# Cross-attention on one Trainium2 core: where the transposition of the probabilities, the third remainder and the key and value loads stand in each slot's order

## Chip, core and metric

The kernel runs on one core of one Trainium2 chip. The metric is the device time of one execution in microseconds (us). TensorE is called PE below (its weight loads PEld), VectorE is DVE, ScalarE is ACT, GpSimd is POOL, and SyncE, which here only issues DMAs, is SP.

## The reference

Only one layer of what the reference sets up is live: cross-attention of `x` (32 batches of 512 rows of 640 channels) with the 77 context rows of each batch, 20 heads of 32 channels, a softmax over the 77 keys, an output projection, a bias and a residual. The three other key sets have no rows here (the context ends at row 77), so they add nothing.

```python
ehs_txt = encoder_hidden_states[:, :77]
q = _heads(hidden_states @ to_q_w)
h_txt = _sdpa(q, _heads(ehs_txt @ to_k_w), _heads(ehs_txt @ to_v_w))
out = _merge(h_txt) @ to_out_w + to_out_b
out = out + hidden_states
```

All of it is float32. The kernel splits each operand into a high part (rounded to the type that PE takes) and a low part (the remainder), and adds up high x high, high x low and low x high.

## The kernel before

A first stage (about the first 300 us) makes keys and values of all batches and puts them into DRAM (`k_dram`, `v_dram`). The main stage is 160 slots, five for each of the 32 batches. Slot `n = 5 b + j` treats chunk `j` of batch `b`: 128 channels, which are four heads. Below, "slot 0" to "slot 4" are the five values of `j`. The order of the instructions is written out by hand: each engine runs its own in the order of the program, and so does SP with the DMAs.

What one slot does:

- **Scores.** Four times (`t` = 0 to 3, 128 query rows each) PE makes scores for four heads (L367: one matmul with the high queries and two with arranged copies, `qt` slots 1 and 2, of low and high halves), and DVE takes the negated row maximum (L375, `nm`). Score banks are three deep. `exps` (L385) has ACT make sixteen exponentials in four groups of four, with row sums.
- **Queries of the next slot.** PE makes them in two parts (L332; 6 and 9 matmuls) into the single bank `pq`. `split_q` has ACT copy the high part (L343) and then two half copies of it from SBUF (L347); DVE subtracts to get the low part (L349, two instructions), which waits for L343 alone. The next slot's second and third score matmuls need L349; the bank `pq` is free only after it.
- **Probabilities of the slot before.** DVE makes reciprocals of the sums (L395), POOL multiplies (`normalize`, L400), DVE transposes in blocks of 32 into `z` (`transpose_p`, L407; one buffer), and SP writes `z` to DRAM with four DMAs (L414, `pd<-z`). One slot later `load_p` reads it back with two DMAs (L423, L424, `raw<-pd`), which completes the transposition. So L407 of a slot waits until the four `pd<-z` of the slot before have landed, and `load_p` waits for the same.
- **Values, three slots behind** (`taken`). ACT casts the loaded probabilities to the high part (`cast_p`, L431) and a third tile of 64 rows (`rest_p`, L437); DVE subtracts for the low part (L438), POOL for the third tile (`last_p`, L445). PE then makes eight matmuls (`values`, L459): the first needs L431, the second L438, the last two L437 and L445. `split_a` splits the result on ACT and DVE (L104, L105).
- **Output projection of an earlier batch**: twice twelve matmuls (`piece`, L489). `finish` has DVE add a closed half to the residual (L517), and SP write a row block out (L521) when both halves are closed. Residuals are loaded by L478, the bias is added by POOL (L482).
- **Loads.** `refill` loads keys in slots 0 and 2 (L309 and L312, eight DMAs) and values in slots 1 and 3 (L319, seven DMAs), half of them at the slot's start and half after `load_p`. In slot 4 `load_x` loads the `x` of the batch after next (L267, four DMAs). `x` is transposed on DVE (L272) and split on ACT and POOL (L279, L280) in slots 2 and 3.

Where the change touches it, the order before is, engine by engine:

- SP: first half of the refill; `load_p`; second half; `out` of the first `finish`; `load_x` (slot 4); residual; four `pd<-z`; `out` of the second `finish`.
- POOL: `normalize`; `last_p`; bias; splits of `x`.
- DVE: maximum 0; L438; L395; maximum 1; L517; maximum 2; **L407; L349 twice**; maximum 3; L517; L105.
- ACT: L431; L437; exponentials 0; exponentials 1; L343; L347 twice; exponentials 2; splits of `x`; L104; exponentials 3.

The program gives its DMAs eight completion semaphores in turn. An issue on SP waits until the transfer that was issued eight places before it has landed, whatever that one was.

Of the kernel before, what the change touches and what calls it, by code (L numbers as in the profile page):

```python
# [35 lines left out]
SEGMENTS = []  # L36
# [14 lines left out]
def kernel(  # L51
# [251 lines left out]
    def load_keys(b, g, heads=range(HPC)):  # L303
        j0, nj = GROUPS[g]
        kb, kc = kbs[g]
        src = k_dram[:, j0 : j0 + nj, :, b * NKEY : (b + 1) * NKEY].bitcast(F32)
        for i in heads:
            r, half = slice(i * HD, (i + 1) * HD), i % 2 * NKEY
            nc.sync.dma_start(  # L309
                kb[r, :, i * NKEY : (i + 1) * NKEY].bitcast(F32), src[r, :, i // 2, :]  # L310
            )
            nc.sync.dma_start(kc[r, :, :, half : half + NKEY].bitcast(F32), src[r])  # L312

    def load_values(b, g, segments=SEGMENTS):
        j0, nj = GROUPS[g]
        v = v_dram.rearrange("n (j i) d a -> n j i (d a)", i=HPC)
        for t, r0, i, k0, kn in segments:
            k0 += b * NKEY
            nc.sync.dma_start(  # L319
                vbs[g][r0 : r0 + kn, :, t, i * HD : (i + 1) * HD, :]  # L320
                .rearrange("p j d a -> p j (d a)")
                .bitcast(F32),
                v[k0 : k0 + kn, j0 : j0 + nj, i, :].bitcast(F32),
            )
# [28 lines left out]
    def scores(n, t):  # L353
        b, j = divmod(n, NC_)
        g = GROUP_OF[j]
        qt, (kb, kc) = qts[n % 2], kbs[g]
        jg = j - GROUPS[g][0]
        sc = ps.tile([P, S], F32, tag="sc", name="sc", bufs=3)
        half = KCOLS // 2
        for m, (cols, keys_) in enumerate(  # L360
            (
                (slice(0, KCOLS), kb[:, jg]),
                (slice(0, half), kc[:, jg, 0]),
                (slice(half, KCOLS), kc[:, jg, 1]),
            )
        ):
            nc.tensor.matmul(  # L367
                sc[:, cols],
                qt[:, m, t * P : (t + 1) * P],
                keys_,  # L370
                start=(m == 0),
                stop=(m == 2),
            )
        nm = main.tile([P, HPC], F32, tag="nm", name="nm", bufs=3)
        nc.vector.tensor_reduce(  # L375
            nm, sc[:, :KCOLS].rearrange("p (h k) -> p h k", k=NKEY), AX.X, ALU.max, negate=True
        )
        return sc, nm

    def exps(n, t, sc, nm):  # L380
        if t == 0:
            sms[n] = main.tile([P, NQ * HPC], F32, tag="sm", name="sm", bufs=2)
        for i in range(HPC):
            at = t * HPC + i
            nc.scalar.activation(  # L385
                pnb[n % 2][:, at, :NKEY],
                sc[:, i * NKEY : (i + 1) * NKEY],
                AF.Exp,
                bias=nm[:, i : i + 1],
                accum_out=sms[n][:, at : at + 1],  # L390
            )

    def sums(n):
        rs = main.tile([P, NQ * HPC], F32, tag="rs", name="rs", bufs=2)
        nc.vector.reciprocal(rs, sms.pop(n))  # L395
        return rs

    def normalize(n, rs):
        pf = pnb[n % 2][:, :, :NKEY]
        nc.gpsimd.tensor_tensor(  # L400
            pf, pf, rs.unsqueeze(2).to_broadcast([P, NQ * HPC, NKEY]), ALU.mult
        )

    def transpose_p(n):

        pn = pnb[n % 2]
        nc.vector.transpose(  # L407
            z.rearrange("p b t j -> p t b j"),
            pn.rearrange("p (t h) k -> p t (h k)", t=NQ).rearrange("p t (b i) -> p t b i", i=Q),
        )  # L410
        pd = dram.tile([NBLK * Q, S], F32, tag="pd", name="pd", bufs=6)
        rows = pd.rearrange("(b i) q -> i b q", i=Q)
        for a in range(4):
            nc.sync.dma_start(  # L414
                rows[:, :, a * P : (a + 1) * P],
                z[a * Q : (a + 1) * Q].rearrange("p b t j -> p b (t j)"),
            )
        pds[n] = pd
# [8 lines left out]
    def cast_p(n):  # L427

        raw = raws[n]
        pp = late[0].tile([P, 5, S], FPR, tag="pp", name="pp", bufs=1)  # L430
        nc.scalar.copy(pp[:, 0:2, :], raw[:, 0:2, :])  # L431
        pps[n] = pp

    def rest_p(n):

        raw, pp = raws[n], pps[n]
        nc.scalar.copy(pp[:64, 4, :], raw[:64, 2, :])  # L437
        nc.vector.tensor_tensor(  # L438
            pp[:, 2:4, :], raw[:, 0:2, :], pp[:, 0:2, :].bitcast(F32), ALU.subtract
        )  # L440

    def last_p(n):

        raw, pp = raws.pop(n), pps[n]
        nc.gpsimd.tensor_tensor(  # L445
            pp[64:, 4, :], raw[:64, 2, :], pp[:64, 4, :].bitcast(F32), ALU.subtract
        )
# [27 lines left out]
    def load_residual(b, t, xr=None):  # L475
        if xr is None:
            xr = late[0].tile([P, C], F32, tag="xr", name="xr", bufs=3)
        nc.sync.dma_start(xr, x[b, t * P : (t + 1) * P, :])  # L478
        xrs[b, t] = xr
# [31 lines left out]
    def finish():  # L511

        while closed:
            b, t, h = closed.pop(0)
            xr = xrs[b, t]
            cols = slice(h * HALF, (h + 1) * HALF)
            nc.vector.tensor_tensor(  # L517
                xr[:, cols], pos.pop((b, t, h))[:, :HALF], xr[:, cols], ALU.add
            )
            if h == 1:  # L520
                nc.sync.dma_start(out[b, t * P : (t + 1) * P, :], xr)  # L521
# [18 lines left out]
        values(m)  # L540
        split_a(m)

    def refill(b, j, part):

        heads = range(2 * part, 2 * part + 2)
        segments = SEGMENTS[4 * part : 4 * part + 4]
        if j == 0:
            load_keys(b, 1, heads)
        elif j == 1:
            load_values(b, 0, segments)  # L550
        elif j == 2 and b + 1 < B:
            load_keys(b + 1, 0, heads)
        elif j == 3:
            load_values(b, 1, segments)

    def slot(n, beside=None):
        b, j = divmod(n, NC_)
        ahead, more = n + 1 < N, b + 1 < B
        back, first = PIECES[j]
        bo_, has_out = b - back, b >= back  # L560
        xsplits = SPLIT_X.get(j, ((), ())) if more else ((), ())
        turns = TRANSPOSE_X.get(j, ((), (), ())) if more else ((), (), ())
        taken, second = takes.get(n), seconds.get(n)

        refill(b, j, 0)
        if taken is not None:
            cast_p(taken)
        s = scores(n, 0)
        if taken is not None:
            rest_p(taken)  # L570
        if n:
            normalize(n - 1, sums(n - 1))
        if taken is not None:
            last_p(taken)
        exps(n, 0, *s)
        if ahead:
            queries(n + 1, 0, 2)
        s = scores(n, 1)
        if n - LAG + 1 in pds and n > LATE:
            load_p(n - LAG + 1)  # L580
        refill(b, j, 1)
        finish()
        if j == 4 and b + 2 < B:
            load_x(b + 2)
        if j in RESIDUAL and b >= RESIDUAL[j][0]:
            load_residual(b - RESIDUAL[j][0], RESIDUAL[j][1])
        if j in BIAS and b >= BIAS[j][0]:
            add_bias(b - BIAS[j][0], BIAS[j][1])
        exps(n, 1, *s)
        for i in turns[0]:  # L590
            transpose_x(b + 1, i)
        if ahead:
            queries(n + 1, 2, NC_)
        s = scores(n, 2)
        if n:
            transpose_p(n - 1)
        if ahead:
            split_q(n + 1)
        exps(n, 2, *s)
        for c in xsplits[0]:  # L600
            split_x(b + 1, c)
        if has_out:
            piece(bo_, first)
        if taken is not None:
            values(taken)
        if beside:
            beside()
        s = scores(n, 3)
        finish()
        for i in turns[1]:  # L610
            transpose_x(b + 1, i)
        if taken is not None:
            split_a(taken)
        for c in xsplits[1]:
            split_x(b + 1, c)
        exps(n, 3, *s)
        if has_out:
            piece(bo_, first + 1)
        for i in turns[2]:
            transpose_x(b + 1, i)  # L620
        if second is not None:
            cast_p(second)
            rest_p(second)
            last_p(second)
            take(second)
            if second + 2 in pds and second + 2 not in takes.values():
                load_p(second + 2)
# [141 lines left out]
```

## Time and profile before

| | us |
|---|---|
| three runs | 2018.67, 2020.97, 2023.04 |
| median | 2020.97 |
| the profiled execution, its own time | 2018.67 |
| its span, first to last instruction | 2016.9 |

The granted clock of TensorE was 0.989 over the span. The page of the profile gives these busy shares:

| engine | busy us | share of the span | instructions |
|---|---|---|---|
| PE | 1963.4 | 97% | 11012 |
| PEld | 1763.5 | 87% | 11012 |
| ACT | 1588.0 | 79% | 6377 |
| DVE | 1354.7 | 67% | 2159 |
| POOL | 981.9 | 49% | 617 |

The DMA queue of SP moved 421.10 MB, its packets took 82.4% of sixteen engines' span. Durations used below are mean times of one instruction or, where stated, start times in a stretch of the timeline; all times are from the start of the span.

| line, engine | what | count | mean ns |
|---|---|---|---|
| L407 DVE | `z<-pn` | 160 | 1511 |
| L349 DVE | `qt<-pq,qt` | 320 | 670 |
| L375 DVE | `nm<-sc` | 640 | 460 |
| L438 DVE | `pp<-raw,pp` | 160 | 1226 |
| L400 POOL | `pn<-pn,rs` | 160 | 2278 |
| L445 POOL | `pp<-raw,pp` | 160 | 1309 |
| L431 ACT | `pp<-raw` | 160 | 1063 |
| L347 ACT | `qt<-qt` | 320 | 619 |

### The profile page before, as it was taken

What the parts mean: (1) busy time and instruction counts of PE and PEld (TensorE: products, weight loads), DVE (VectorE), ACT (ScalarE), POOL (GpSimd) and SP (SyncE); (2) the same over time, 40 slices, a digit from 0 to 9 for tenths busy, and PEclk for the clock granted to TensorE, in tenths of its full rate; (3) what the DMA queues carried; (4) which work ended last, traced back from release to release, by engine and by line L of the source; (5) the groups of instructions that cost most, each with busy time, mean ns of one, the idle gap of its engine ahead of it and who ended that gap; (6) DMA issues with size and microseconds to landing.
All of it is one profiled execution on the core that took longest, in us unless ns stands there. A gap on an engine that the chain in (4) does not pass through costs nothing.

```text
span 2016.9 us, 38271 instructions
## 1 busy us (share of the span) xinstructions
PE 1963.4 (97%) x11012; PEld 1763.5 (87%) x11012; DVE 1354.7 (67%) x2159; ACT 1588.0 (79%) x6377; POOL 981.9 (49%) x617
## 2 busy tenths in 40 slices
PE   9999997899999999999999999999999999999998
PEld 7889986789888988888898888888888888988898
DVE  4443225777777777777777677777777777777764
ACT  3321128889889988888898899899898889989993
POOL 0000023555555555555556555666555655555554
PEclk9999998999999999999999999999999999999999
DMA  7993366888888888888988888888888888888875
GB/s 172 221 255 108 105 148 151 222 222 221 223 223 220 226 218 226 217 218 218 229 226 220 208 227 229 222 223 218 217 222 219 218 224 218 228 222 222 222 202 169
DMA packets 555997, 423.55 MB, mean 210 GB/s; under 512 B 170191, under 2 KB 459501, under 8 KB 555789
## 3 DMA queue, kind: packets, MB, share of 16 engines
q1 hardware_dynamic: 555789, 421.10, 82.4%
q8 instruction: 91, 1.49, 0.3%
q14 instruction: 117, 0.96, 0.1%
HBM read 245.61 MB, written 175.32 MB: 209 GB/s over the span
## 4 chain that ended last, share of the span: by engine, by line
PE 54%; DMA 19%; SPq 8%; POOL 6%; issue 5%; ACT 4%; DVE 4%; DVEq 0%; POOLq 0%; ACTq 0%
PE pq L332 17%; PE po L489 15%; DMA pd<-z 8%; PE pa L459 8%; PE sc L367 6%; POOL pn L400 4%; PE pv L197 4%; PE pk L168 4%; DMA xs<-in_x_dram 3%; DMA raw<-pd 3%; SPq L414 2%; DVE qt L349 2%; ACT pn L385 2%; POOL pp L445 2%; DMA kb<-k_dram 1%
## 5 line engine op out<-in xcount | busy, mean ns | idle before, releaser
L385 ACT ACTIVATE pn<-sc,nm 128x77 f32<-128x77 f32 x2560 | 799.2, 329 | 109.3 <-DVE nm L375 96.5
L400 POOL TENSOR_TENSOR pn<-pn,rs 128x1232 f32<-128x1232 f32 x160 | 364.5, 2278 | 692.6 <-DVE rs L395 541.2
L489 PE MATMUL po<-wo_s,at 128*128 128x320 f32 x3840 | 627.6, 313 | 1.4 <-DVE xr L517 1.4
L332 PE MATMUL pq<-xt,wq_s 128*128 128x512 f32 x2400 | 622.5, 400 | 0.0
L489 PEld LDWEIGHTS po<-wo_s,at 128*128 128x128 f32 x3840 | 567.0, 189 | 2.0 <-DVE xr L517 1.7
L385 ACT ACTIVATION_READ_ACCUMULATOR pn<-sc,nm 128x1 f32 x2560 | 530.6, 207 | 0.0
L332 PEld LDWEIGHTS pq<-xt,wq_s 128*128 128x128 f32 x2400 | 429.7, 190 | 77.5 <-POOL xt L280 0.2
L375 DVE TENSOR_REDUCE nm<-sc 128x4 f32<-128x308 f32 x640 | 294.0, 460 | 264.3 <-PE sc L367 258.1
L459 PE MATMUL pa<-pp,vb 128*128 128x512 f32 x1280 | 337.7, 402 | 19.6 <-ACT pp L431 9.9
L407 DVE STREAM_TRANSPOSE z<-pn 128x1280 f32<-128x1280 f32 x160 | 241.8, 1511 | 119.2 <-DMA pd<-z 62.4
L459 PEld LDWEIGHTS pa<-pp,vb 128*128 128x128 f32 x1280 | 242.5, 197 | 68.3 <-POOL pp L445 20.7
L367 PEld LDWEIGHTS sc<-kc,qt 128*128 128x128 f32 x1280 | 213.3, 189 | 40.9 <-issue 13.9
L367 PE MATMUL sc<-kc,qt 128*128 128x154 f32 x1280 | 227.1, 256 | 13.6 <-DVE qt L349 12.9
L438 DVE TENSOR_TENSOR pp<-raw,pp 128x1024 fp32r<-128x1024 f32 x160 | 196.2, 1226 | 50.1 <-ACT pp L431 34.3
L445 POOL TENSOR_TENSOR pp<-raw,pp 64x512 fp32r<-64x512 f32 x160 | 209.4, 1309 | 36.4 <-ACT pp L437 24.3
L349 DVE TENSOR_TENSOR qt<-pq,qt 64x512 fp32r<-64x512 f32 x320 | 214.3, 670 | 7.5 <-ACT qt L343 3.1
L280 POOL TENSOR_TENSOR xt<-xs,xt 128x512 fp32r<-128x512 f32 x157 | 199.7, 1299 | 16.8 <-ACT xt L279 12.2
L482 POOL TENSOR_TENSOR xr<-xr,bias 128x640 f32<-128x640 f32 x128 | 201.2, 1573 | 12.0 <-POOL pp L445 2.7
L347 ACT CAST qt<-qt 64x512 fp32r<-64x512 f32 x320 | 198.1, 619 | 9.0
L367 PE MATMUL sc<-kb,qt 128*128 128x308 f32 x640 | 196.0, 306 | 1.2 <-ACT qt L343 1.2
L431 ACT CAST pp<-raw 128x1024 fp32r<-128x1024 f32 x160 | 170.1, 1063 | 1.3 <-DVE at L105 0.8
L104 ACT CAST at<-pa 128x512 fp32r<-128x512 f32 x160 | 94.9, 593 | 75.5 <-PE pa L459 72.8
(41 smaller groups left out, 1536.3 us busy)
## 6 DMA issues: line engine op xcount, KB each, us to landing
pd<-z SPq DMA_DIRECT2D x640, 160.0 KB, 3.6
raw<-pd SPq DMA_DIRECT2D x160, 512.0 KB, 4.1
xs<-in_x_dram SPq DMA_DIRECT2D x128, 320.0 KB, 7.5
xr<-in_x_dram SPq DMA_DIRECT2D x128, 320.0 KB, 3.8
out_dram<-xr SPq DMA_DIRECT2D x128, 320.0 KB, 3.3
raw<-pd SPq DMA_DIRECT2D x160, 128.0 KB, 4.2
v_dram<-vs SPq DMA_DIRECT2D x19, 640.0 KB, 4.0
k_dram<-ks SPq DMA_DIRECT2D x80, 128.0 KB, 2.4
```

Of the source, the lines that this page charges most:

```text
L280: engine.tensor_tensor(parts[1], src, parts[0].bitcast(F32), ALU.subtract)
L332: nc.tensor.matmul(pqs[n], wq_s[:, k, a, j * P : (j + 1) * P], xts[b, k][:, c, :], start=(k == 0 and m == 0), stop=(k == NC_ - 1 and m == 2),)
L349: nc.vector.tensor_tensor(qt[r, 1 + w, :], pq[r], qt[r, 0, :].bitcast(F32), ALU.subtract)
L367: nc.tensor.matmul(sc[:, cols], qt[:, m, t * P : (t + 1) * P], keys_, start=(m == 0), stop=(m == 2),)
L375: nc.vector.tensor_reduce(nm, sc[:, :KCOLS].rearrange("p (h k) -> p h k", k=NKEY), AX.X, ALU.max, negate=True)
L385: nc.scalar.activation(pnb[n % 2][:, at, :NKEY], sc[:, i * NKEY : (i + 1) * NKEY], AF.Exp, bias=nm[:, i : i + 1], accum_out=sms[n][:, at : ...
L400: nc.gpsimd.tensor_tensor(pf, pf, rs.unsqueeze(2).to_broadcast([P, NQ * HPC, NKEY]), ALU.mult)
L407: nc.vector.transpose(z.rearrange("p b t j -> p t b j"), pn.rearrange("p (t h) k -> p t (h k)", t=NQ).rearrange("p t (b i) -> p t b i", i=Q),)
L445: nc.gpsimd.tensor_tensor(pp[64:, 4, :], raw[:64, 2, :], pp[:64, 4, :].bitcast(F32), ALU.subtract)
L459: nc.tensor.matmul(pas[n], vb[:, t, :, a], pp[:, c, :], start=(m == 0), stop=(m == len(PASSES) - 1),)
L482: nc.gpsimd.tensor_tensor(xrs[b, t], xrs[b, t], bias, ALU.add)
L489: nc.tensor.matmul(pos[b, t, h][:, :HALF], ats[b * NC_ + j][:, a, t * P : (t + 1) * P], wos[0][:, j, c, h * HALF : (h + 1) * HALF], start= ...
```

## The change

Three moves; nothing is added or removed.

- `refill` issues all of its loads at the slot's start. `finish` (with its `out`) goes ahead of `load_p`, directly after the second group of scores. So SP's order becomes: whole refill; `out`; `load_p`; `load_x`; residual; four `pd<-z`; `out`.
- `last_p` goes ahead of `normalize`, so POOL makes L445 before L400. DVE's order does not change by it.
- `transpose_p` goes behind `split_q` and the third group of exponentials, so DVE makes L349 twice and then L407. The place of the four `pd<-z` on SP does not change.

`split_q` itself is the same before and after.

```diff
-    def refill(b, j, part):
-
-        heads = range(2 * part, 2 * part + 2)
-        segments = SEGMENTS[4 * part : 4 * part + 4]
+    def refill(b, j):
+
         if j == 0:
-            load_keys(b, 1, heads)
+            load_keys(b, 1)
         elif j == 1:
-            load_values(b, 0, segments)
+            load_values(b, 0)
         elif j == 2 and b + 1 < B:
-            load_keys(b + 1, 0, heads)
+            load_keys(b + 1, 0)
         elif j == 3:
-            load_values(b, 1, segments)
+            load_values(b, 1)
...
-        refill(b, j, 0)
+        refill(b, j)
         if taken is not None:
             cast_p(taken)
         s = scores(n, 0)
         if taken is not None:
             rest_p(taken)
+            last_p(taken)
         if n:
             normalize(n - 1, sums(n - 1))
-        if taken is not None:
-            last_p(taken)
         exps(n, 0, *s)
         if ahead:
             queries(n + 1, 0, 2)
         s = scores(n, 1)
+        finish()
         if n - LAG + 1 in pds and n > LATE:
             load_p(n - LAG + 1)
-        refill(b, j, 1)
-        finish()
...
         s = scores(n, 2)
-        if n:
-            transpose_p(n - 1)
         if ahead:
             split_q(n + 1)
         exps(n, 2, *s)
+        if n:
+            transpose_p(n - 1)
```

## The prediction

> **What bounds the kernel now.** I read the busy shares first (PE 97%), then cut the span at the first score matmul of each slot. One batch from slot 1 to slot 0 (length, then busy time of PE, PEld, DVE, ACT, POOL):
>
> ```profile
> 1360.85:1372.10 11.25, 10.82 (x61) 9.34 (x60) 10.37 (x18) 9.62 (x43) 3.56 (x2) 1.00 0.80 208
> 1372.10:1382.41 10.31, 10.31 (x61) 9.35 (x60) 8.74 (x14) 10.08 (x43) 7.04 (x5) 1.00 0.83 226
> 1382.41:1392.74 10.33, 10.33 (x61) 9.37 (x60) 7.02 (x12) 10.19 (x42) 7.86 (x6) 1.00 0.76 209
> 1392.74:1403.07 10.33, 10.33 (x62) 9.37 (x61) 7.81 (x13) 9.31 (x41) 6.85 (x5) 1.00 0.87 213
> 1403.07:1413.37 10.30, 10.30 (x61) 9.33 (x60) 4.34 (x7) 8.01 (x32) 5.13 (x3) 1.00 0.97 218
> ```
>
> Four slots of five are PE without a gap, 10.32 us each; slot 1 is longer, on average over all batches 11.30. So a batch takes about 52.55 where PE alone needs 5 x 10.32 = 51.6, and about 0.95 x 30 = 28 us in all is lost, each time in slot 1. The waits (engine, line, releaser: us in total, times, longest) name it:
>
> ```profile
> DVE z L407 <- DMA pd<-z: 62.4, 23, 4.0
> ...
> PEld pa L459 <- POOL pp L445: 20.7, 30, 2.4
> ...
> PE sc L367 <- DVE qt L349: 12.9, 30, 1.6
> ...
> PE pa L459 <- POOL pp L445: 8.4, 25, 2.0
> ...
> SPq L312 <- DMA xs<-in_x_dram: 42.6, 31, 2.2
> ```
>
> Thirty times, once a batch, PE waits for L349 and for L445. Both are late because L407 of slot 0 waits for the `pd<-z` of slot 4, which are queued behind 1.3 MB of `x`. The last line matters for the change: key loads have nothing to do with `x`, yet wait for it, through the eight semaphores. DVE in slot 0 of that batch:
>
> ```profile
> 1358.50 1.52 DVE L407 STREAM_TRANSPOSE z<-pn 128x1280 f32<-128x1280 f32 x1 [2.76 <-DMA pd<-z]
> 1359.93 1.37 DVE L349 TENSOR_TENSOR qt<-pq,qt 64x512 fp32r<-64x512 f32 x2
> 1361.33 0.48 DVE L375 TENSOR_REDUCE nm<-sc 128x4 f32<-128x308 f32 x1
> ```
>
> Call T the landing of the last `pd<-z` of slot 4 (here just before 1358.50). L349 and the fourth maximum are stuck behind it, then exponentials 3, then the cast of slot 1. Next, SP at the following such place, and ACT:
>
> ```profile
> 1401.34 3.64 SPq L414 DMA_DIRECT2D pd<-z  x4
> 1405.08 1.14 SPq L521 DMA_DIRECT2D out_dram<-xr  x1
> 1406.66 0.30 SPq L309 DMA_DIRECT2D kb<-k_dram  x1
> 1408.37 0.30 SPq L312 DMA_DIRECT2D kc<-k_dram  x1
> 1408.92 1.20 SPq L309 DMA_DIRECT2D kb<-k_dram  x1
> 1410.17 0.42 SPq L312 DMA_DIRECT2D kc<-k_dram  x1
> 1411.67 0.38 SPq L423 DMA_DIRECT2D raw<-pd  x1
> ```
> ```profile
> 1416.54 1.05 ACT L431 CAST pp<-raw 128x1024 fp32r<-128x1024 f32 x1
> ```
>
> `load_p` is issued 0.13 us after T (1411.54), and the cast of slot 1 begins 0.08 after its data land (1416.46). So there is a loop as long as a batch: cast of slot 1, ACT's work to the cast of slot 3, L407 of slot 3, its `pd<-z`, `load_p` of slot 4, behind it in the DMA queue `x`, the residual and `pd<-z` (that is T), `load_p` of slot 0, cast of slot 1. From issue and landing times of 28 batches, means: 9.51 (cast 1 to 2) + 10.15 (to 3) + 6.45 (to the end of L407) + 0.74 (to the first `pd<-z` issue) + 2.56 (to the end of the fourth) + 3.16 (landing) + 0.14 (to `load_p`) + 15.06 (to T) + 0.13 (to `load_p`) + 4.09 (landing) + 0.55 (to the cast) = 52.54. Only the 0.55 is slack.
>
> **L349 ahead of L407.** Same three instructions. L349 waits for L343 alone, which ACT begins 4.11 us after the cast and ends at 4.70; so L349 runs from 4.75 to 6.12 (1.37) and L407 ends at 7.65, where it ended at 6.45: +1.20 in the loop. In slot 0 the gain is plain: L349 ends long before T, so PE's wait for it goes (12.9 us), and exponentials 3 come 1.37 earlier: T + 0.17 + 1.52 + 0.5 + 1.35 = T + 3.6 in place of T + 4.8. The later L407 is partly hidden: SP was not free for its `pd<-z` until 0.74 after it, and no refill stands between `load_p` and them any more. I take 0.10 for 0.74 (bounds 0.05, 0.74), 2.42 for the four issues (2.36 to 3.13 seen), 3.00 for landing (2.83 to 4.01). Together +0.28.
>
> **L445 ahead of L400.** L445 began at cast + 5.0, behind L400 and so behind L395; now at cast + 1.62, when L437 is done. PE's waits for it (20.7 + 8.4, partly the same time) go. L400 was ready at cast + 2.65 and now waits for L445, so it ends near cast + 5.3 in place of 4.91; the next user, L407, is not ready before 6.12, so this costs nothing. Without L349 in front it would cost 0.4 a slot.
>
> L445 now runs beside L438. The trace has five such places, at the start and the end:
>
> ```profile
> 343.77 1.75 POOL L445 TENSOR_TENSOR pp<-raw,pp 64x512 fp32r<-64x512 f32 x1 [6.28 <-ACT pp L437]
> ```
> ```profile
> 343.16 1.23 DVE L438 TENSOR_TENSOR pp<-raw,pp 128x1024 fp32r<-128x1024 f32 x1 [2.33 <-ACT pp L431]
> ```
>
> 1.75 in place of a median of 1.29, with L438 unhurt. So L445 ends at cast + 3.37 and L400 at 5.68, still 0.44 ahead of L407: nothing. The Trainium skill ("SBUF — State Buffer", section "Who interferes with whom") says that a DVE instruction with both inputs in SBUF shuts out a GpSimd instruction that reads SBUF until it ends. By that rule L445 would be an estimated 1.91 and L400 would end at 5.84: dearer than the row, and still hidden.
>
> **Whole refill and `out` ahead of `load_p`.** In slot 0 eight key loads now stand there. The fifth to eighth wait, by the semaphores, for the second, third and fourth `pd<-z` and for `out`. `out` lands 0.82 after T (mean), the eighth issue takes 0.43, the step to `load_p` 0.05: `load_p` at T + 1.30 in place of T + 0.13. Bounds: 0.13, if all eight slip into the wait for T, and 1.75 (`out` at 0.94 and two slow issues). I take 1.30, since the third and fourth loads above already went out only as `x`, residual and `pd<-z` landed. Its landing was 4.09 (3.46 to 4.88); with `out` gone from the queue but four key loads ahead I take 3.95. The cast then begins at T + 5.35, where ACT is ready at T + 3.6, so the slack 0.55 shrinks to 0.10.
>
> In slots 1 to 3 `load_p` also moves behind three or four issues of about 0.5, and in 1 and 2 behind `out`, which waits for L517. What it delays is the cast a slot later. The data lie ready 1.91, 1.99 and 2.61 us (medians) before the casts of slots 2, 3 and 4; in slot 1 I get 1.2 later. Hidden. Without this cover each would cost the same 1 to 2 us as slot 0.
>
> **Sum.** 9.51 + 10.15 + 7.65 + 0.10 + 2.42 + 3.00 + 0.14 + 15.06 + 1.30 + 3.95 + 0.10 = 53.38, +0.84 a batch. Over 29 laps +24 us: 2018.67 + 24 = 2043 on the profiled execution, 2020.97 + 24 = 2045 on the median; I say 2044. So PE's old waits go, PE loses 53.4 - 51.6 = 1.8 a batch to a new one, and the loop that was just covered sets the time.
>
> **Rivals.** *The loads slip in under T* (faster). If `load_p` stays at T + 0.13, the loop is 53.38 - 1.17 = 52.21, -0.33 a batch: 2009; with a short landing and fast `pd<-z` as well it falls under PE's 51.6, and -0.94 x 29 gives 1992. For it: SP idles between key loads. Against: that idle time is itself the wait for landings. *The raw load is hit twice* (slower still): key bytes ahead of it take its landing to the 4.88 seen at worst, and the late `load_p` of slot 1 comes to decide; 54.3 a batch, 2071. For it: the DMA share of 0.97 in slot 0. Against: the bytes are the same, only reordered. *It nets out*: the terms cancel, 52.4 to 52.65, 2020. For it: +1.20 and -1.37 are the same two instructions. Against: they lie in different slots, and only +1.20 is on the loop.
>
> **How the numbers follow.** Forecast 56% (52.7 to 54.0 a batch, 2025 to 2061), slower still 16%, nets out 8%, faster 20%. A measurement of this kernel tells about 0.2%, 4 us, from no change. So slower 72%, same 8%, faster 20%. The range leaves a tenth out on each side: half of the faster case below 2004, the worse half of the slower below the top, 2066.
>
> **What would show it.** Right: L423 of slot 0 about 1.3 after T; ACT's L431 waiting about 1.7 a batch for `raw<-pd`, 50 us in all, where it waited 0.2; no PE wait for L445 in the main stage; L445 near 1.75; L407 ending 7.65 after the cast of slot 3. Wrong: L423 still 0.13 after T, or slot 1 no longer than the others, which would put the batch at 51.6.

## The result and the profile after

The changed kernel is slower: 2076.14 us (median of four runs, 2070.88 to 2080.92) against 2022.01 (median of four, 2018.67 to 2023.85) on the same chip. The ratio is 1.0269, 95% interval 1.0233 to 1.0305, that is +54 us where +24 was forecast; the time lies above the range that was given (2066). The profiled execution took 2080.43, its span is 2078.6, the granted clock 0.983 (0.989 before).

One batch of the changed kernel, cut at the first score matmul of slots 1, 2, 3, 4 and 0 as before (length; busy time of PE, PEld, DVE, ACT, POOL; granted clock; DMA share; GB/s):

```profile
1401.40:1412.05 10.65, 10.62 (x61) 9.29 (x60) 7.89 (x15) 7.46 (x31) 4.03 (x2) 1.00 0.60 168
1412.05:1422.36 10.31, 10.31 (x62) 9.35 (x60) 9.15 (x15) 9.48 (x43) 4.88 (x3) 1.00 0.75 204
1422.36:1435.39 13.03, 10.60 (x62) 9.38 (x60) 8.97 (x15) 12.37 (x49) 9.99 (x8) 1.00 0.85 238
1435.39:1445.71 10.32, 10.32 (x61) 9.36 (x60) 7.69 (x13) 9.78 (x44) 8.14 (x6) 1.00 0.83 219
1445.71:1456.02 10.31, 10.31 (x62) 9.34 (x60) 5.56 (x9) 8.19 (x34) 5.62 (x3) 1.00 1.07 235
```

The long slot is now slot 3 (12.31 us on average over 28 batches, slot 1 10.84). PE has the same work (10.6 busy) and stands still for 2.4 us in it. The list of PE's waits of the changed kernel, and one line of ACT's, say for what (engine, line, releaser: us in total, times, longest):

```profile
PE po L489 <- DVE xr L517: 53.9, 29, 5.0
...
PE sc L367 <- DVE qt L349: 2.3, 5, 0.6
```
```profile
ACT pp L431 <- DMA raw<-pd: 91.3, 55, 4.1
```

The old waits are gone: L349 cost PE 12.9 us in thirty places and now 2.3, and L445 is not in PE's list any more. In their place PE waits once a batch for L517, which stands behind late work on DVE. In the slot 3 above:

```profile
1430.94 1.39 DVE L349 TENSOR_TENSOR qt<-pq,qt 64x512 fp32r<-64x512 f32 x2 [1.50 <-ACT qt L343]
...
1434.30 0.88 DVE L517 TENSOR_TENSOR xr<-po,xr 128x320 f32<-128x320 f32 x2
```
```profile
1434.84 0.71 PE L489 MATMUL po<-wo_s,at 128*128 128x320 f32 x3 [2.43 <-DVE xr L517]
```

L349 waits for ACT's L343, which begins 4.05 us after the cast of the slot, and L407, a maximum and L517 follow L349 on DVE. Why the cast is late is in the second fence of the waits: ACT now waits for the loaded probabilities (91.3 us, 0.2 in all before; the prediction named 50 as a sign). Of the 55 waits 31 are in slot 1, 9 in slot 2 and 15 in slot 3. The three casts after one T (1400.28 here) in the timeline of ACT:

```profile
1405.80 1.05 ACT L431 CAST pp<-raw 128x1024 fp32r<-128x1024 f32 x1 [1.95 <-DMA raw<-pd]
1415.66 1.05 ACT L431 CAST pp<-raw 128x1024 fp32r<-128x1024 f32 x1 [0.35 <-DMA raw<-pd]
1426.26 1.05 ACT L431 CAST pp<-raw 128x1024 fp32r<-128x1024 f32 x1 [0.53 <-DMA raw<-pd]
```

These are slots 1, 2 and 3, and in this batch each of them waits, not the first alone. SP over the same stretch:

```profile
1401.60 0.30 SPq L312 DMA_DIRECT2D kc<-k_dram  x1
1402.00 0.39 SPq L423 DMA_DIRECT2D raw<-pd  x1
1402.43 0.48 SPq L424 DMA_DIRECT2D raw<-pd  x1
1403.00 2.91 SPq L414 DMA_DIRECT2D pd<-z  x4
1405.95 4.46 SPq L319 DMA_DIRECT2D vb<-v_dram  x7
1410.53 0.53 SPq L521 DMA_DIRECT2D out_dram<-xr  x1
1411.15 0.39 SPq L423 DMA_DIRECT2D raw<-pd  x1
...
1421.35 0.36 SPq L521 DMA_DIRECT2D out_dram<-xr  x1
1421.81 0.38 SPq L423 DMA_DIRECT2D raw<-pd  x1
```

L423 of slot 0 is issued 1.72 after T, behind the eighth key load, which waited for `out`. That is the place that was forecast. But in slot 1 the four `pd<-z` had landed at 1408.50, and L423 comes only at 1411.15, behind seven value loads (4.46 us) and `out`; in slot 2 they had landed at 1420.22, and L423 comes at 1421.81. DVE in slot 0 of the changed kernel, to set beside the three lines of before:

```profile
1396.21 1.41 DVE L349 TENSOR_TENSOR qt<-pq,qt 64x512 fp32r<-64x512 f32 x2
1400.45 1.51 DVE L407 STREAM_TRANSPOSE z<-pn 128x1280 f32<-128x1280 f32 x1 [2.84 <-DMA pd<-z]
1402.00 0.48 DVE L375 TENSOR_REDUCE nm<-sc 128x4 f32<-128x308 f32 x1
```

L349 no longer stands behind the wait for T, as forecast. The group of L445 on the page:

```profile
L445 POOL TENSOR_TENSOR pp<-raw,pp 64x512 fp32r<-64x512 f32 x160 | 280.8, 1755 | 640.8 <-ACT pp L437 594.1
```

The loop of the prediction, term by term, means over the same 28 batches (us):

```
                                         before  forecast  after
cast of slot 1 to cast of slot 2           9.51      9.51   9.67
cast of slot 2 to cast of slot 3          10.15     10.15  10.43
cast of slot 3 to end of L407              6.45      7.65   7.67
to the first pd<-z issue                   0.74      0.10   0.03
to the end of the fourth issue             2.56      2.42   2.52
to their landing                           3.16      3.00   3.08
to load_p of slot 4                        0.14      0.14   0.14
to T                                      15.06     15.06  14.92
T to load_p of slot 0                      0.13      1.30   1.41
to its landing                             4.09      3.95   4.54
to the cast of slot 1                      0.55      0.10   0.08
sum                                       52.54     53.38  54.48
```

The terms follow one another round the loop, so they add up to a batch whatever bounds it; the sum alone proves nothing. That the loop sets the time shows in the steps without slack: `pd<-z` 0.03 after L407, `load_p` of slot 4 0.14 to 0.16 after the landing, the cast of slot 1 0.08 after its data, in all of the 28 batches. The two profiled executions differ by 61.7 us of span, about 53 of them in these batches (1.94 each by the sums), the rest ahead of and behind them. Of the 1.10 that the forecast is short, 0.59 is the landing in slot 0, 0.44 the casts from slot 1 to 3, and 0.11 the issue; the other terms take off 0.04.

### The profile page after: what moved, and what is told of

The parts are those of the page before. It is cut to its first block, busy times and chain, and to the rows that moved or that the text cites. A ratio compares the mean times of both kernels' runs of the same rounds, so it can differ in the third digit from the quotient of the medians.

```text
span 2078.6 us, 38304 instructions
## 1 busy us (share of the span) xinstructions
PE 1977.9 (95%) x11012; PEld 1774.1 (85%) x11012; DVE 1350.7 (65%) x2159; ACT 1586.7 (76%) x6377; POOL 1048.8 (50%) x617
## 4 chain that ended last, share of the span: by engine, by line
PE 37%; DMA 18%; ACT 14%; DVE 11%; SPq 7%; issue 6%; POOL 2%; DVEq 0%; ACTq 0%; POOLq 0%
PE pq L332 11%; PE po L489 9%; DMA raw<-pd 7%; ACT pn L385 7%; PE pa L459 5%; PE pv L197 4%; DVE z L407 4%; PE pk L168 4%; PE sc L367 4%; DMA pd<-z 3%; ACT pp L431 3%; SPq L319 3%; SPq L414 3%; DMA out_dram<-xr 3%; DVE nm L375 2%
## 5 line engine op out<-in xcount | busy, mean ns | idle before, releaser
L489 PE MATMUL po<-wo_s,at 128*128 128x320 f32 x3840 | 635.9, 314 | 53.9 <-DVE xr L517 53.9
L332 PE MATMUL pq<-xt,wq_s 128*128 128x512 f32 x2400 | 630.3, 404 | 0.0
L445 POOL TENSOR_TENSOR pp<-raw,pp 64x512 fp32r<-64x512 f32 x160 | 280.8, 1755 | 640.8 <-ACT pp L437 594.1
L332 PEld LDWEIGHTS pq<-xt,wq_s 128*128 128x128 f32 x2400 | 435.0, 192 | 78.8 <-POOL xt L280 0.2
L400 POOL TENSOR_TENSOR pn<-pn,rs 128x1232 f32<-128x1232 f32 x160 | 364.5, 2278 | 42.5 <-DVE rs L395 30.3
L438 DVE TENSOR_TENSOR pp<-raw,pp 128x1024 fp32r<-128x1024 f32 x160 | 196.1, 1226 | 220.2 <-ACT pp L431 220.2
L407 DVE STREAM_TRANSPOSE z<-pn 128x1280 f32<-128x1280 f32 x160 | 241.9, 1512 | 72.0 <-DMA pd<-z 48.3
L349 DVE TENSOR_TENSOR qt<-pq,qt 64x512 fp32r<-64x512 f32 x320 | 220.2, 688 | 96.2 <-ACT qt L343 91.5
L431 ACT CAST pp<-raw 128x1024 fp32r<-128x1024 f32 x160 | 169.7, 1061 | 92.3 <-DMA raw<-pd 91.3
L367 PEld LDWEIGHTS sc<-kc,qt 128*128 128x128 f32 x1280 | 214.5, 191 | 25.3 <-ACT qt L347 3.6
L197 PE MATMUL pv<-wv_s,ct 128*128 128x320 f32 (+1 forms) x960 | 144.9, 313 | 3.0 <-DVE vs L105 3.0
```

Of the source, the lines that this page charges most:

```text
L197: nc.tensor.matmul(pv[:tn, :HALF], cts[k][:, a, t0 : t0 + tn], wv_s[:, k, c, h * HALF : (h + 1) * HALF], start=(k == 0 and n == 0), stop=( ...
L332: nc.tensor.matmul(pqs[n], wq_s[:, k, a, j * P : (j + 1) * P], xts[b, k][:, c, :], start=(k == 0 and m == 0), stop=(k == NC_ - 1 and m == 2),)
L349: nc.vector.tensor_tensor(qt[r, 1 + w, :], pq[r], qt[r, 0, :].bitcast(F32), ALU.subtract)
L367: nc.tensor.matmul(sc[:, cols], qt[:, m, t * P : (t + 1) * P], keys_, start=(m == 0), stop=(m == 2),)
L400: nc.gpsimd.tensor_tensor(pf, pf, rs.unsqueeze(2).to_broadcast([P, NQ * HPC, NKEY]), ALU.mult)
L407: nc.vector.transpose(z.rearrange("p b t j -> p t b j"), pn.rearrange("p (t h) k -> p t (h k)", t=NQ).rearrange("p t (b i) -> p t b i", i=Q),)
```

## The experiments

They ran on other chips, where the kernel before took 2033 to 2039 us, so ratios are compared, each against the kernel before on its own chip. That kernel was not profiled there; at 0.5 to 0.8% more time its batch would be an estimated 0.3 to 0.4 us longer than 52.54, so a few tenths between traces of different chips mean little.

**One move at a time.** On the kernel before, SP's move alone:

```diff
         refill(b, j, 0)
+        refill(b, j, 1)
...
         s = scores(n, 1)
+        finish()
         if n - LAG + 1 in pds and n > LATE:
             load_p(n - LAG + 1)
-        refill(b, j, 1)
-        finish()
```

> Of the three moves this has SP's alone: whole refill and the first finish ahead of load_p; POOL and DVE keep their old order. Loop theory: load_p of slot 0 goes from 0.13 to about 1.35 us after T, its landing from 4.09 to 4.5, the slack of 0.55 before the cast of slot 1 is used up, and the four pd<-z follow L407 of slot 3 about 0.65 sooner since no refill is in their way: 52.54 + 1.2 + 0.45 - 0.47 - 0.65 = 53.1 a batch, 2039 us (2030 to 2050), about a third of the loss of the whole change. Rival, that the late L407 in every slot does the damage: this run stays at 2022 within 6. Second rival, that the reordered bytes alone do it: nearly the whole loss, 2065 or more.

Measured: 1.0114 (1.0080 to 1.0147). By its ratio within what the loop theory allowed, and neither rival's number; by its terms not quite: 53.78 a batch where 53.1 was expected, `load_p` 1.29 after T and its landing 4.47 as forecast, but casts 1 to 3 are 0.74 longer than before, which the expectation left out.

POOL's move alone:

```diff
             rest_p(taken)
+            last_p(taken)
         if n:
             normalize(n - 1, sums(n - 1))
-        if taken is not None:
-            last_p(taken)
```

> Of the three moves this has POOL's alone: last_p ahead of normalize; SP and DVE keep their old order. Loop theory: L445 beside L438 takes 1.75, L400 ends at cast + 5.7 in place of 4.9, and L407, L349 and the fourth maximum, all behind it on DVE, come 0.8 later; where ACT has little else (slots 0, 1, 4) the next cast follows about 10.3 after the last in place of 9.5, so slot 1 cannot catch up and the batch becomes about 0.8 longer: 2045 us (2030 to 2055). Rival, that the wait for L445 was what cost PE its time in slot 1: half of the 0.95 a batch comes back, 2008 us.

Measured: 1.0124 (1.0101 to 1.0146). The cast of slot 2 follows that of slot 1 after 10.41 and the cast of slot 3 after 10.42, where it was 9.51 and 10.15. L445 is early and PE does not wait for it, but the L407 behind L400 takes L349 and the maximum along (L407 ends 7.36 after the cast of slot 3 in place of 6.45). The long slot is slot 3 here too (11.98), with 39.8 us of PE's waits for L517.

DVE's move alone:

```diff
-        if n:
-            transpose_p(n - 1)
         if ahead:
             split_q(n + 1)
         exps(n, 2, *s)
+        if n:
+            transpose_p(n - 1)
```

> Of the three moves this has DVE's alone: L349 twice ahead of L407; SP and POOL keep their old order. Loop theory: L407 of slot 3 ends 7.65 after the cast in place of 6.45, its pd<-z follow it at once (0.1 in place of 0.74), and the cast of slot 1 now waits for the data alone, so the slack of 0.55 falls to 0.08: 52.54 + 1.20 - 0.64 - 0.47 = 52.6 a batch, 2023 us (2012 to 2032). Rival, that the late L407 in every slot does the damage: 2050 or more. Rival, that PE's wait for L349 is what costs: 0.43 a batch comes back, 2009.

Measured: 1.0063 (1.0036 to 1.0090), a little above what the loop theory allowed. The `pd<-z` followed L407 after 0.45, not 0.1: with the refill halved, SP was not free. None of the rivals' numbers came out.

POOL's and DVE's moves together (the last two edits):

> POOL's and DVE's moves together; SP keeps its old order, so against the changed kernel this undoes SP's move alone. Loop theory: load_p of slot 0 is issued 0.13 after T again and lands 4.1 later, and PE waits for neither L445 nor L349. 9.45 + 10.14 + 7.65 + 0.1 + 2.5 + 3.1 + 0.14 + 15.0 + 0.13 + 4.1 + 0.08 = 52.4 a batch: 2018 us (2005 to 2028), so SP's move is worth 55 of the changed kernel's loss. Rival, that the DVE order makes every slot late: above 2045. Rival, that the loop does not bind without SP's move: PE's 51.6, 1994.

Measured: 1.0032 (1.0013 to 1.0051), 53.23 a batch, just above what was expected. So the two moves, which cost 1.2% and 0.6% alone, cost 0.3% together: L349 ahead of L407 is what hides the late L400, as the prediction said when it priced the cover. Nearly all of the loss of the whole change comes with SP's move: 2.7% with it, 0.3% without. The moves do not add up: SP's costs 1.1% on the kernel before and 2.4% on top of the other two. The traces suggest why. The cast of slot 3 comes 23.93 after T with POOL's and DVE's moves, 24.44 before them; with SP's move it comes at 26.22 without them and at 26.08 with them, since late data hold the casts of slots 1 to 3 in many batches. So what the two moves gain ahead of that cast is lost, while L407 still ends 1.2 later behind it.

**SP's move taken apart, on the changed kernel.** Slot 0 put back:

```diff
-    def refill(b, j):
+    def refill(b, j, part=0):

         if j == 0:
-            load_keys(b, 1)
+            load_keys(b, 1, range(2 * part, 2 * part + 2))
...
             load_p(n - LAG + 1)
+        if j == 0:
+            refill(b, j, 1)
```

> The changed kernel with one thing undone: in slot 0 the last four key loads stand behind load_p again; slots 1 to 3 keep the whole refill. Loop theory: load_p of slot 0 goes back from 1.41 to 0.13 us after T, its landing from 4.54 to about 4.4, so a batch goes from 54.48 to about 53.05; against the kernel before this gives a ratio of 1.006 (1.000 to 1.013), where the whole change has 1.027. Rival, that the refills of slots 1 to 3 and their late loads carry the loss (casts 1 to 3 are 0.44 longer): 1.018 or more.

Measured: 1.0278 (1.0247 to 1.0309): nothing came back; the rival's number came out. `load_p` of slot 0 is at T + 0.13 again and the cast of slot 1 at T + 4.60, but the casts of slots 1 and 2 are now 11.39 apart in place of 9.67. The cast of slot 2 waits for its own data in every batch.

`finish` put back behind `load_p`:

```diff
-        finish()
         if n - LAG + 1 in pds and n > LATE:
             load_p(n - LAG + 1)
+        finish()
```

> The changed kernel with finish behind load_p again; the refills stay whole. In slots 1 and 2 load_p no longer waits for out, and so not for L517. Loop theory: slot 0 has no out there, so its 1.41 and 4.54 stay; only the late loads of slots 1 and 2 (casts 1 to 3, 0.44 a batch too long) gain, at most 0.44: ratio 1.020 to 1.025. Rival, that waiting for out is the main cost of SP's move: 1.012 or less.

Measured: 1.0265 (1.0232 to 1.0297), no gain either. `out` ahead of `load_p` is not the cost by itself: the casts of slots 1 to 3 are 0.63 nearer together than in the changed kernel (19.47 us from the first to the third), but from the cast of slot 3 to the next T it is 0.89 longer (29.25).

The places of the three loads and casts, from T, show why (us, means over 28 batches). "Landed" is the `pd<-z` of the slot before, which `load_p` waits for; "its data" is the landing of what this `load_p` loads, which the cast of the next slot needs. The columns are of four chips (before and changed of one, POOL+DVE of a second, slot 0 of a third, the last two of a fourth):

```
                          before  POOL+DVE  changed  slot 0  slots 0, 1  slots 0-2
                                   (no SP)            old       old         old
slot 0  load_p              0.13      0.13     1.41    0.13      0.13        0.13
slot 1  cast                4.78      4.58     5.98    4.60      4.57        4.45
slot 1  pd<-z landed        8.21      8.30     8.38    8.32      8.32        8.14
slot 1  load_p              8.40      8.50    10.77   10.90      8.52        8.36
slot 1  its data           12.47     12.70    15.23   15.91     12.70       12.57
slot 2  cast               14.29     14.02    15.65   15.99     14.06       13.85
slot 2  pd<-z landed       18.01     18.34    19.09   19.25     18.33       18.22
slot 2  load_p             18.25     18.52    21.23   20.79     20.68       18.36
slot 2  its data           22.39     22.85    25.86   25.94     25.96       22.64
slot 3  cast               24.44     23.93    26.08   26.38     26.06       23.77
next T                     52.54     53.21    54.44   54.69     54.58       53.73
```

There are three ways from T to the cast of slot 3: by the data for the cast of slot 1, of slot 2 or of slot 3. With 9.44 and 9.91 from cast to cast (POOL+DVE, where ACT's work sets them) and 0.08 from data to cast, the three give 23.9, 22.7 and 22.9 in the kernel with POOL's and DVE's moves, and 25.3, 25.2 and 25.9 in the changed one: SP's move makes all three late, to within 0.7 of each other. The two columns on the right are the test of that: `SPLIT` is (0, 1) in the first of these runs and (0, 1, 2) in the second, and `refill` with `None` issues all its loads:

```diff
-        refill(b, j)
+        refill(b, j, 0 if j in SPLIT else None)
...
-        finish()
+        if j not in SPLIT:
+            finish()
         if n - LAG + 1 in pds and n > LATE:
             load_p(n - LAG + 1)
+        if j in SPLIT:
+            refill(b, j, 1)
+            finish()
```

> The changed kernel with SP's old order (halved refill, finish behind load_p) in slots 0 and 1 alone; whole refill in slots 2 and 3. Undoing slot 0 alone gave nothing, because load_p of slots 1 and 2 were late by as much. If there are three nested paths from T to the cast of slot 3 (by the data of slots 1, 2 and 3), the third is still long here: load_p of slot 2 about 2 after its pd<-z, data at T + 25, cast of slot 3 at T + 25.1 where SP's old order has 23.9: about 54.2 a batch, ratio 1.017 (1.011 to 1.023). Rival, that only the paths through slots 0 and 1 count: 53.3, ratio 1.003 to 1.008.

Measured: 1.0207 (1.0167 to 1.0248), as the theory had it. The cast of slot 3 is at T + 26.06, held by its data alone.

> The changed kernel with SP's old order in slots 0, 1 and 2; the whole refill stands ahead of load_p in slot 3 alone, whose data are wanted in the next slot 4, outside the loop. Nested-path theory: all three paths are short again, 53.2 to 53.5 a batch, ratio 1.005 (1.001 to 1.010), so that three undone together give what one alone does not. Rival, that the refill of slot 3 counts too, by the pd<-z that it holds back: 1.013 or more.

Measured: 1.0077 (1.0050 to 1.0104). With slots 0, 1 and 2 undone together, most of the loss is gone; slot 0 alone gave nothing, slots 0 and 1 a quarter. So the loss lies in SP's order in slots 0 to 2 taken together; slots 1 and 2 were not undone one at a time, and how much is the refill's and how much `out`'s was not parted further. What is left over POOL's and DVE's moves (1.0077 against 1.0032) comes behind the cast of slot 3: from there to the next T it is 29.96 in place of 29.28, and the landing of slot 3's `pd<-z` takes 3.68 in place of 3.20.

**`load_p` ahead of everything.** The changed kernel with this order on SP:

```diff
-        refill(b, j)
...
         if n - LAG + 1 in pds and n > LATE:
             load_p(n - LAG + 1)
+        refill(b, j)
+        finish()
```

> The changed kernel with load_p ahead of the whole refill and of finish in every slot, so no key or value bytes and no issue stand between pd<-z and load_p. Loop theory: load_p 0.13 after T and a landing near 3.7, since nothing but out is queued ahead; the refill fills the time behind it: 9.4 + 9.95 + 7.65 + 0.3 + 2.45 + 3.2 + 0.14 + 15.1 + 0.13 + 3.7 + 0.08 = 52.1 a batch, ratio 0.993 (0.986 to 1.000). Rival, that the refill issued later pushes the four pd<-z of the slot back by as much as it gained: 1.003 or more, as with SP's old order.

Measured: 1.1175 (1.1136 to 1.1214), far beyond even the rival. SP in this kernel:

```profile
1535.43 0.38 SPq L423 DMA_DIRECT2D raw<-pd  x1
...
1541.92 2.62 SPq L414 DMA_DIRECT2D pd<-z  x4
1547.12 0.38 SPq L423 DMA_DIRECT2D raw<-pd  x1
1547.55 0.47 SPq L424 DMA_DIRECT2D raw<-pd  x1
1548.11 4.13 SPq L319 DMA_DIRECT2D vb<-v_dram  x7
1552.28 0.60 SPq L478 DMA_DIRECT2D xr<-in_x_dram  x1
1552.98 2.51 SPq L414 DMA_DIRECT2D pd<-z  x4
...
1558.94 0.38 SPq L423 DMA_DIRECT2D raw<-pd  x1
```

Here is a second loop, as long as a slot: four `pd<-z` (2.5), landing (3.2), `load_p` (0.9), and whatever SP issues from there to the next `pd<-z` (5). From L423 to L423 that is 11.7 and 11.8 here, over the 10.32 of PE; on average 11.7 to 15.1 in four of the five slots, and 10.30 only from slot 0 to slot 1. The forecast gave `pd<-z` 0.3 after L407; it was 4.29. What stands ahead of `load_p` delays its data, what stands behind it delays the next `pd<-z`; the halved refill of the kernel before seems to share the cost between the two.

**The burst of `x`.** The changed kernel, the kernel before, and POOL's and DVE's moves alone, each with `load_x` moved to behind `transpose_p` and the third group of exponentials:

```diff
-        if j == 4 and b + 2 < B:
-            load_x(b + 2)
...
+        if j == 4 and b + 2 < B:
+            load_x(b + 2)
```

> The changed kernel with the four loads of x in slot 4 behind that slot's four pd<-z in place of ahead of them; all else as changed. Loop theory: the 15 us between load_p of slot 4 and T hold nearly 7 of x; without them T comes 5 or more earlier, the loop has slack, and PE's 51.6 a batch bounds: ratio 0.985 (0.978 to 0.995), though everything else of the change stays. Rival, that the change loses by late L407 or by the issues on SP as such: it stays above 1.015. Second rival, that x then comes too late for its transposition in slot 0: L272 waits and the batch is as long as before, 1.00 to 1.01.

Measured: 1.0645 (1.0606 to 1.0684). From `load_p` of slot 4 to T it is now 10.09 in place of 14.92, but `load_p` of slot 0 comes 8.56 after T in place of 1.41: the key loads ahead of it wait, by the semaphores, for `x`.

> The kernel before with one move of its own: the four loads of x in slot 4 stand behind that slot's pd<-z. In slot 0 only four key loads stand between x and load_p, and of these one waits for x, so load_p should issue near 5.6 us of slot 0 (7.9 before) and z is free early. Loop theory: T comes about 5 us sooner, L407 of slot 0 no longer waits, PE's loss in slot 1 (0.95 a batch) goes: ratio 0.987 (0.981 to 0.996). Rival, seen in the run with x behind in the changed kernel: loads that wait by the semaphores for x hold load_p back, and the ratio is above 1.01.

Measured: 1.0021 (0.9999 to 1.0043), not to be told from no change. L407 of slot 0 no longer waits, but `load_p` is 4.25 after T and its landing takes 6.90 in place of 4.09, since `x` is ahead of it in the queue. The cast of slot 1 still comes late (2.87 into its slot, 2.26 in the kernel before).

> POOL's and DVE's moves of the change, SP's old order, and the four loads of x behind the pd<-z of slot 4. Loop theory: T comes 5 sooner and load_p of slot 0 is held by one key load alone; with the later L407 its issue is near 6.5 of slot 0 (9.9 without the move of x). The loop gains 2 or more and has slack under PE's 51.6: ratio 0.986 (0.980 to 0.996). Rival, that the x transfers ahead of the data of slot 0 in the queue give it all back: 1.000 or more.

Measured: 1.0114 (1.0086 to 1.0142); the same, with a landing of 7.01. Both expectations were wrong: moved as a whole, `x` stays on the loop. Next it was parted, two of the four loads in the old place and two behind `load_p` of the next slot 0, with the first block transposition of `x` in slot 1 (`load_x` now takes the quarters to load):

```diff
         if n - LAG + 1 in pds and n > LATE:
             load_p(n - LAG + 1)
+        if j == 0 and b and b + 1 < B:
+            load_x(b + 1, range(2, 4))
...
         if j == 4 and b + 2 < B:
-            load_x(b + 2)
+            load_x(b + 2, range(2))
...
-    TRANSPOSE_X = {0: ((), (0,), ()), 1: ((1,), (2,), ()), 2: ((3,), (), ())}
+    TRANSPOSE_X = {1: ((0,), (1, 2), ()), 2: ((3,), (), ())}
```

On the kernel before:

> The kernel before, with two of the four loads of x where they were in slot 4 and the other two behind load_p of the next slot 0; the first block transposition of x moves from slot 0 to slot 1. Loop theory: T comes 3.4 sooner (two x transfers of 1.7), L407 of slot 0 hardly waits, the data of slot 0 land near 8.7 of that slot, and the other two transfers land before slot 1 needs x: PE's loss of 0.95 a batch goes, ratio 0.986 (0.981 to 0.994). Rival: x lands too late for slot 1 or holds back pd<-z of slot 0, ratio 1.00 or more.

Measured: 0.9978 (0.9961 to 0.9995). A gain, but a sixth of what was expected: T comes 3.3 sooner after `load_p` of slot 4 (11.75), and the casts of slots 1 and 2 are then 11.36 apart, since `pd<-z` of slot 0 land behind the other half (T + 11.4) and L407 of slot 1 waits for them (27 times, 42.0 us in all).

With POOL's and DVE's moves:

> POOL's and DVE's moves of the change, SP's old order, and x in two halves as above. Loop theory: 53.2 less 3.4 is under PE's 51.6 a batch, so PE bounds: ratio 0.985 (0.980 to 0.993), no better than without these moves. Rival: with the later L407 the stretch from slot 3 on stays long, 1.00 or more.

Measured: 0.9948 (0.9928 to 0.9968), a third of the gain expected, but faster than both kernels. PE's longest wait is again

```profile
PE po L490 <- DVE xr L518: 24.8, 21, 5.0
```

(L517 of the other kernels, one line further down), less than half of what it is after the whole change. PE's 51.6 a batch is not reached (52.57).

With the whole change:

> The whole change, with x in two halves as above. Loop theory: T comes up to 3.4 sooner on every lap, the three paths from T to the cast of slot 3 stay as long as they are (26 us), so the batch goes from 54.4 to between 51.6 (PE) and 52.5: ratio 0.993 (0.984 to 1.006), and the change as such costs little without the burst. Rival, that late issues and the late L407 cost by themselves: 1.015 or more.

Measured: 1.0117 (1.0095 to 1.0140), between the theory and its rival. So more than half of the loss goes with half of the burst, but the late issues still cost: `load_p` of slot 1 is at T + 13.27, and 1.4 after its `pd<-z`.

## Why the prediction was right in direction and too small

**Right.** The loop, the term that the change lengthens first (T to `load_p` of slot 0, 1.30 forecast, 1.41 measured), the end of L407 (7.65 and 7.67 after the cast of slot 3), the partial hiding of the late L407 (`pd<-z` at once, 0.03), the end of PE's waits for L349 and L445, and L445 at 1.75 beside L438 at no cost as long as L349 stands in front of L407 (L407 waited for L400 91 times before, 38.2 us, and twice after, 5.6). The cost of that cover's loss was shown by POOL's move alone: 1.2%, with the end of L407 0.91 later, where the prediction said 0.4 a slot. Two sums of the prediction are slightly off and change nothing: "+0.28" is 0.26, and "T + 3.6" is 3.54.

**The step that failed: the word "hidden" for slots 1 to 3.** The prediction put the cost of SP's move in these slots at nothing. It had the late `load_p` of slots 1, 2 and 3 covered, "in slot 1 I get 1.2 later. Hidden", from data that lay ready 1.9 us and more before their cast. Measured, `load_p` of slot 1 went from T + 8.40 to 10.77, 2.4 later, and of slot 2 from 18.25 to 21.23, and the data from 12.47 to 15.23 and from 22.39 to 25.86. So the data came 2.76 and 3.47 later, more than the 1.91 and 1.99 that covered them, and the casts of slots 1 to 3 lie 0.44 further apart. Of 29 batches, 12 casts in slot 2 and 22 in slot 3 begin as soon as the data land. Three things were missed. In slot 1 the seven value loads take 4.46 us in the batch shown (median of such groups 4.45), more than the half microsecond each that was reckoned, and `out` comes behind them. The landing is longer too: from `load_p` to its data 4.46 and 4.63 in slots 1 and 2, where it was 4.07 and 4.14. And the delays add up along the way: a later cast makes a later L407 and later `pd<-z`, and `load_p` of the next slot waits for these. The three ways are now of about one length, so that the loss cannot be had back by the first of them (slot 0 undone 1.0278, slots 0 and 1 1.0207, slots 0 to 2 1.0077). This is the step that decides: with slot 0 undone `load_p` is at T + 0.13 and lands in 4.39, less than the prediction allowed for the two, and the batch is still 54.69.

**Also wrong, in size: the landing in slot 0.** 3.95 was taken, 4.54 came on average and 5.60 at worst, over the bound of 4.88. Four runs on one other chip give 4.17 with POOL's move alone, 4.33 with DVE's, 4.39 with both and 4.47 with SP's alone. So part of it comes without the keys ahead of the data. The kernel before was not profiled on that chip, and what part is the chip's stays open.

**The rivals.** "The raw load is hit twice" had the right second place, the late `load_p` of slot 1, but gave it 16% and 2071; 2076 is its case. "The loads slip in under T" and "it nets out" are excluded by the issue at T + 1.41. PE's new wait was forecast as a size (1.8 a batch; 54.48 - 51.6 = 2.9 came), without its place, which is L517 in slot 3. The sign that was to show the prediction wrong, slot 1 no longer than the others, therefore could not tell: slot 1 is 10.84 and slot 3 12.31, yet the batch is far from 51.6. The place goes with POOL's move (slot 3 is the longest slot with it alone, 11.98; slot 1 with SP's alone, 12.30, and with DVE's alone, 12.39), the length of the batch with the loop.

## What to carry to other kernels

Where one engine issues all DMAs in the order of the program, as SP does here, a load's place is priced twice: what is issued ahead of it delays its data, and what is issued behind it delays the next store, so find both loops before moving anything. A delay is hidden only if the slack stays: after the first late step, reckon the slack of the following ones anew, because several ways of about equal length turn a small move into a loss that undoing one of them need not give back. Where two orders on two engines depend on each other (here L400 and L349 around L407), test them together, since each alone can cost more than both (1.2% and 0.6% alone, 0.3% together).

## What was not expected of the hardware

A group of seven small loads (8 to 60 KB) took SP 4.46 us to issue in one place of the changed kernel, and 1.89 for three in one of the kernel before, 0.64 and 0.63 each. In neither place was it the semaphores: the transfer eight places before each of these loads had landed before its issue began. What makes an issue last 0.43 to 0.86 us there, and 0.30 for key loads elsewhere on the same queue, is not shown. Moving 1.3 MB of `x` behind four stores made the changed kernel 3.7% slower (1.0645 against 1.0269), where eight key loads that share the semaphores stand between it and `load_p`, and left the time of the kernel before alone (1.0021), where four do.

L445 takes 1.755 us beside L438 in place of 1.29, in 155 of its 160 runs, while L438 stays at 1.226. It begins 0.61 after L438, so 0.62 of L438 is left when it begins, and it loses 0.46: less than if it were shut out for all of the rest.
